# A graph-attention layer and a masked attention layer on one core: where the first layer's result is turned, which sums the q, k, v products share, and when the adjacency is copied and loaded

## The chip, the cores and the metric

The kernel runs on one core of a Trainium2 chip. The metric is the device time of one execution in microseconds; lower is better. The core has a matrix engine (TensorE, PE in the profile, with its weight loads shown as PEld), a vector engine (VectorE, DVE), a scalar engine (ScalarE, ACT), GpSimd (POOL) and SyncE (SP), which here only issues transfers. Each engine takes its own instructions in order. Transfers are done by 16 shared DMA engines.

## The reference

There are N = 4096 nodes with D = 512 features, and a 0/1 adjacency matrix of 4096 x 4096, about 0.8% of it ones. Two layers are applied, each with a residual and a layer norm:

```python
# layer 0: 4 heads of width 128
support = (x @ weight) by heads
w    = leaky_relu(f1 + f2, 0.2)          # f1, f2: dot products of support with weight_u, weight_v
attn = softmax over j of w where adjacency is set
x    = layernorm(x + attn @ support + bias + x @ proj_w + proj_b)

# layer 1: 8 heads of width 64
q, k, v = x @ Wqs, x @ Wks, x @ Wvs
scores  = q k^T / 8, masked by adjacency with the diagonal set
x       = layernorm(x + softmax(scores) v Wo)
```

Everything is float32.

## The kernel before, in words

The program has four stages one after the other. TensorE is in use through all of them.

**First products (0 to about 210 us of the span).** x is loaded in groups of 512 rows, turned by VectorE in blocks of 32 x 32 (line 741: `nc.vector.transpose`), and multiplied by the two weight matrices. Since a turn in blocks of 32 leaves the features in another order over the partitions, the weights are loaded in the same order (`load_w0`).

**Layer 0 (about 210 to 1136 us).** The 4096 result rows are taken in four windows w of 1024; for each window there is a pass for each head h, and each pass has 32 units j of 128 source rows. A unit is one trip of the loop at line 1065. In it VectorE makes a tile p of 128 x 1024 weights (`front`, line 641, and, for every second unit, a bitwise AND of mask and signs at line 636, whose signs z come from ScalarE, line 625), and TensorE multiplies the eight 128-column parts of p by the head's support rows (line 1076, 16 records in a unit). `front` runs LA = 3 units ahead of the products, and p has LA + 1 = 4 buffers. z has two buffers of two units each.

Beside that runs the preparation of the next window's adjacency (`beside_unit`; u = 32 h + j counts the units of a window):
- `narrow(w + 1, c)`, a copy in DRAM of one eighth of the window from float32 to bfloat16, issued from GpSimd (line 589) after a small token that VectorE writes, which ties it to the unit;
- `turn_in0(w + 1, c)`, a transposing load of that eighth from SyncE (line 595) into `stage`, which has two buffers;
- `shrink`, four ScalarE copies to 8-bit (line 601), which free `stage`;
- `keep`, a store of the mask to DRAM for layer 1 (line 606).

In the first window `narrow` comes at u = 22 + 7c and the loads at 52 + 8c; in the later ones at 16 + 8c and 44 + 9c. `shrink` follows its load by 14 to 18 units. SyncE's queue also holds, at j = 6 of each pass, the next pass's `fr_t` and eight `sup_t` loads (lines 616 and 987, 1 MB and 2 MB).

When a window's last pass ends, its rows are closed while the next window is already running: `divide`, `add_base`, then `close` (line 1043) for the eight row tiles, at steps 12 + 3t/2 after the end (12 + 2t for the last window). A close is `bn_stats` and `bn_aggr` on VectorE (lines 511 and 513), four small GpSimd operations, and six steps later a ScalarE `normalise` and a store to `x1_d`. Eight steps after `close` (eleven in the last window) comes `turn` (line 1054): four TensorE transposes of 128 x 128 against an identity (line 1057), a ScalarE copy out of PSUM (line 1062) and a store to `x1T_d`. In the last window's passes, groups 0 and 1 of that turned result are loaded (`load_xT`), and the k weights (`load_w`).

**q, k, v (1136 to about 1434 us).** For each pair of 512-row groups (four pairs) and each of k, q, v, `gemm` multiplies a 2 x 2 block matrix of weights by a 2 x 2 block matrix of features with seven products instead of eight. Operands are sums of blocks (`of_weights`, `of_features`), and the four results are sums of the products. A product takes 3.44 us of TensorE. The products accumulate in `s_ps`, which has three buffers. Before, three of the products are copied out by ScalarE (`sb`), GpSimd makes four sums of them in each gemm (line 1214), VectorE does one copy and two final sums (lines 1238, 1245, 1253), and GpSimd makes the features' five sums for the next pair (line 1160). The scale 1/8 of the scores is put on the q weights by one ScalarE operation (line 1273).

**Layer 1 (1434 to 3348 us).** For each group of 512 query rows and each pair of heads: scores (line 1127), exp on ScalarE (line 1341), mask on VectorE (line 1344), products with v (line 1389), sums on GpSimd and by accumulating transfers (lines 1364, 1374). In the last v gemm three scores are made ahead of time (line 1227), ahead of the last product.

The schedule is written out by hand: nothing reorders instructions. `later.at(n, fn)` emits fn n steps on.

Of the kernel before, what the change touches and what calls it, by code (L numbers as in the profile page):

```python
# [18 lines left out]
P = 128  # L19
# [410 lines left out]
def tile_gat_then_masked_attention(  # L430
# [59 lines left out]
    x1_d = [dram.tile([P, D], F32, name=f"x1_d{i}") for i in range(NT)]  # L490
# [6 lines left out]
    x1T_d = [dram.tile([P, KC, G], F32, name=f"x1T_d{g}") for g in range(NG)]  # L497
# [43 lines left out]
    def wait_by_tile(name, bufs, **kw):  # L541
# [16 lines left out]
    order = (2, 3, 4, 5, 1, 6, 7)  # L558
    of_weights = {1: ((0, 0), (1, 1), ALU.add), 2: ((1, 0), (1, 1), ALU.add),
                  5: ((0, 0), (0, 1), ALU.add), 6: ((1, 0), (0, 0), ALU.subtract),  # L560
                  7: ((0, 1), (1, 1), ALU.subtract)}
    of_features = {1: ((0, 0), (1, 1), ALU.add), 3: ((0, 1), (1, 1), ALU.subtract),
                   4: ((1, 0), (0, 0), ALU.subtract), 6: ((0, 0), (0, 1), ALU.add),
                   7: ((1, 0), (1, 1), ALU.add)}
    plain_weights = {3: (0, 0), 4: (1, 1)}
    plain_features = {2: (0, 0), 5: (1, 1)}
# [3 lines left out]
    with tc.tile_pool(name="l0", bufs=NG) as l0, \  # L570
# [21 lines left out]
        def turn_in0(w, c):  # L592

            stage[w, c] = adjT_p.tile([P, CJ, W], BF16, name="stage", bufs=2)
            nc.sync.dma_start_transpose(stage[w, c], adj_d[w][c])
# [359 lines left out]
        xTs = {}  # L955

        def load_w(dst, src, c):
            nc.sync.dma_start(dst[:, c], src[:, c * P:(c + 1) * P, :].rearrange("h p k -> p h k"))

        def load_xT(g, pool=turn_p):  # L960
            xTs[g] = pool.tile([P, KC, G], F32, name="xT1", bufs=2)
            nc.sync.dma_start(xTs[g], x1T_d[g])
# [6 lines left out]
        with wait_by_tile("l0v", 2) as vp:  # L969
            pools[1] = vp, vp  # L970

            def beside_unit(w, h, j):
# [16 lines left out]
                if w + 1 < NW:  # L989
                    for c in range(NCJ):  # L990
                        first, step = (44, 9) if w else (52, 8)
                        if u == (16 + 8 * c if w else 22 + 7 * c):
                            narrow(w + 1, c)
                        if u == first + step * c:
                            turn_in0(w + 1, c)
                        if u == min(first + 20 + step * c, H0 * NT - 1):
                            keep(w + 1, c)
                        if w == 0 and u == 98 + 3 * c:
                            keep(0, c)
                        for k in range(CJ):  # L1000
                            if u == first + 14 + step * c + 4 * k // 3:
                                shrink(w + 1, c, k)
                elif u % 4 == 0 and NT <= u < NT + 4 * KC:
                    load_w(wk, wks, (u - NT) // 4)
                elif u == NT + 4 * KC + 16:
# [576 lines left out]
```

## Time and profile before

The medians and lines are from three timed runs and one profiled execution.

| what | value |
|---|---|
| median of 3 runs (lowest to highest) | 3350.9 us (3349.1 to 3351.21) |
| profiled execution, its own time | 3350.18 us |
| its span, first to last instruction | 3348.4 us |
| mean granted TensorE clock | 0.998 |
| TensorE busy | 3325.1 us, 99% of the span |
| VectorE, ScalarE, GpSimd busy | 70%, 59%, 66% |
| chain that ended last, layer 0's products (L1076) | 27.1% |
| the same, layer 1's products (L1389) and scores (L1127) | 25.9% and 25.8% |
| the same, q, k, v (L1192 and L1185) | 5.5% and 2.7% |
| the same, TensorE's turn of the first layer's result (L1057) | 0.4% |

A busy share is an average over the stages. What an edit is worth is read from the stage that it is in: which engine has no gap there, and what is ready how long before it is needed. Times of matmuls in the profile overlap, since they are pipelined; what one of them adds to the sequence is read from the chain, where each piece starts where the one before it ends.

### The profile page before, as it was taken

What the parts mean: (1) busy time and instruction counts of PE and PEld (TensorE: products, weight loads), DVE (VectorE), ACT (ScalarE), POOL (GpSimd) and SP (SyncE); (2) the same over time, 40 slices, a digit from 0 to 9 for tenths busy, and PEclk for the clock granted to TensorE, in tenths of its full rate; (3) what the DMA queues carried; (4) which work ended last, traced back from release to release, by engine and by line L of the source; (5) the groups of instructions that cost most, each with busy time, mean ns of one, the idle gap of its engine ahead of it and who ended that gap; (6) DMA issues with size and microseconds to landing.
All of it is one profiled execution on the core that took longest, in us unless ns stands there. A gap on an engine that the chain in (4) does not pass through costs nothing.

```text
span 3348.4 us, 66683 instructions
## 1 busy us (share of the span) xinstructions
PE 3325.1 (99%) x27096; PEld 1953.1 (58%) x27096; DVE 2359.6 (70%) x2894; ACT 1986.6 (59%) x2463; POOL 2218.8 (66%) x1588
## 2 busy tenths in 40 slices
PE   9999999999999999999999999999999999999998
PEld 8899999999999755643333333333333333333332
DVE  6689899898999611167776667676666666667676
ACT  1366977878776421256666656566565656656564
POOL 5631040040020365589999999999999999999996
PEclk9999999999999999999999999999999999999999
DMA  8988869589531443379899998889988889887984
GB/s 181 229 191 163 241 152 200 145 197 186 149 105 64 117 160 114 135 204 211 199 209 220 223 208 187 212 195 245 212 191 211 192 204 255 189 211 187 212 195 112
DMA packets 399054, 620.41 MB, mean 185 GB/s; under 512 B 166672, under 2 KB 247568, under 8 KB 397712
## 3 DMA queue, kind: packets, MB, share of 16 engines
q0 software_dynamic: 97520, 258.77, 42.5%
q1 hardware_dynamic: 299344, 354.26, 34.8%
q8 instruction: 215, 3.52, 0.4%
q10 hardware_dynamic: 1872, 3.02, 0.3%
q14 instruction: 103, 0.84, 0.1%
HBM read 315.87 MB, written 117.64 MB: 129 GB/s over the span
## 4 chain that ended last, share of the span: by engine, by line
PE 96%; POOL 1%; DVE 1%; issue 1%; DMA 1%; ACT 0%; SPq 0%; POOLq 0%; ACTq 0%; DVEq 0%
PE o_ps L1076 27%; PE o_ps L1389 26%; PE s_ps L1127 26%; PE s_ps L1192 5%; PE o_ps L847 4%; PE s_ps L1453 3%; PE s_ps L1185 3%; PE s_ps L1408 1%; PE x_ps L1057 0%; DMA p<-p 0%; DVE p L1521 0%; POOL q_sum L1364 0%; POOL s L700 0%; PE x_ps L1185 0%; DVE prod L818 0%
## 5 line engine op out<-in xcount | busy, mean ns | idle before, releaser
L1364 POOL TENSOR_TENSOR q_sum<-q_sum,p 128x1024 f32<-128x1024 f32 x538 | 1374.9, 2556 | 63.0 <-DMA p<-p 39.2
L1344 DVE TENSOR_TENSOR p<-s_ps,adjT 128x1024 f32<-128x1024 f32 x896 | 1043.8, 1216 | 465.3 <-ACT s_ps L1341 436.5
L1341 ACT ACTIVATE s_ps<-s_ps 128x1024 f32<-128x1024 f32 x1021 | 967.1, 1006 | 594.5 <-PE s_ps L1127 594.3
L1389 PE MATMUL o_ps<-p,v_sb 64*64 64x512 f32 x8192 | 943.6, 590 | 0.0
L1127 PE MATMUL s_ps<-q_sb,k_sb 64*64 64x512 f32 x8192 | 942.8, 589 | 0.2 <-DVE p L1344 0.2
L1076 PE MATMUL o_ps<-sup_t,p 128*128 128x129 f32 x8192 | 919.4, 275 | 1.2 <-DVE p L641 1.2
L1076 PEld LDWEIGHTS o_ps<-sup_t,p 128*128 128x128 f32 x8192 | 917.0, 192 | 1.6 <-DVE p L641 1.4
L641 DVE SCALAR_TENSOR_TENSOR p<-fr_t,dj,az 128x1024 f32<-128x1024 f32 x512 | 652.8, 1284 | 80.4 <-PE o_ps L1076 53.1
L1389 PEld LDWEIGHTS o_ps<-p,v_sb 64*64 64x64 f32 x8192 | 310.3, 133 | 570.6 <-issue 560.3
L1127 PEld LDWEIGHTS s_ps<-q_sb,k_sb 64*64 64x64 f32 x8192 | 312.8, 133 | 566.1 <-issue 456.1
L625 ACT ACTIVATE z<-fr_t,f 128x1024 fp8e4<-128x1024 f32 x512 | 558.0, 1144 | 119.4 <-DVE az L636 119.0
L1374 POOL DMA_DIRECT2D p<-p x412 | 437.2, 1297 | 10.2 <-PE o_ps L1389 8.5
L1040 POOL DMA_DIRECT2D agg<-base_d x32 | 28.7, 1206 | 516.0 <-ACT agg L1026 515.8
L1344 DVE TENSOR_TENSOR p<-s_ps,md 128x1024 f32<-128x1024 f32 x128 | 150.7, 1217 | 68.3 <-ACT s_ps L1341 63.6
L588 POOL COPY seen<-token 128x1 f32<-128x1 f32 x24 | 13.6, 565 | 252.9 <-DVE token L586 252.9
L636 DVE TENSOR_TENSOR az<-adjT,z 128x512 int32<-128x512 int32 x256 | 175.5, 686 | 2.1 <-ACT z L625 1.4
L1199 ACT ACTIVATE sb<-s_ps 128x1024 f32<-128x1024 f32 x35 | 35.8, 1024 | 192.6 <-PE s_ps L1192 129.8
L601 ACT ACTIVATE adjT<-stage 128x1024 fp8e4<-128x1024 bf16 x128 | 130.6, 1051 | 9.5 <-DMA stage<-adj_d 9.5
L1214 POOL TENSOR_TENSOR sb<-sb,sb 128x1024 f32<-128x1024 f32 x36 | 84.9, 2373 | 72.2 <-ACT sb L1199 72.2
L1238 DVE COPY k_sb<-s_ps 128x1024 f32<-128x1024 f32 x12 | 14.7, 1225 | 141.0 <-PE s_ps L1192 91.3
L1453 PE MATMUL s_ps<-wo_sb,on 128*128 128x512 f32 x240 | 110.8, 604 | 0.0
L1423 ACT ACTIVATE r<-r_h 32x256 f32<-32x256 f32 x248 | 102.3, 412 | 2.9
(179 smaller groups left out, 2139.4 us busy)
## 6 DMA issues: line engine op xcount, KB each, us to landing
p<-p POOLq DMA_DIRECT2D x412, 512.0 KB, 9.0
k_sb<-k_d SPq DMA_DIRECT2D x128, 512.0 KB
v_sb<-v_d SPq DMA_DIRECT2D x128, 512.0 KB
adj_d<-in_adj_dram POOLq DMA_DIRECT2D x32, 1024.0 KB, 10.9
sup_t<-sup_d SPq DMA_DIRECT2D x120, 258.0 KB
fr_t<-fr_d SPq DMA_DIRECT2D x16, 1024.0 KB
adjT_d<-adjT SPq DMA_DIRECT2D x32, 512.0 KB
adjT<-adjT_d SPq DMA_DIRECT2D x32, 512.0 KB
```

Source lines behind the costliest of these rows:

```text
L625: nc.scalar.activation(z[:, k, :], fr_t[w, h][:, 0, :], AF.Sign, bias=fs[j // GT][:, 0, (j + k) % GT, h:h + 1], saturate=False)
L636: nc.vector.tensor_tensor(az.bitcast(I32), adjT[w, j // CJ][:, j % CJ:j % CJ + 2, :].bitcast(I32), z.bitcast(I32), op=ALU.bitwise_and)
L641: nc.vector.scalar_tensor_tensor(p, fr[:, 1, :], dj[j // GT][:, j % GT, h:h + 1], az_t[w, h, j // 2][:, j % 2, :], op0=ALU.max, op1=ALU.mult)
L1076: nc.tensor.matmul(o[t // BK][:, t % BK, :], p[:, t * P:(t + 1) * P], s, start=(j == 0 and t % BK == 0), stop=(j == NT - 1), skip_group_ch ...
L1127: nc.tensor.matmul(s[c:c + MS, e, :], k[r, a + c:a + c + MS], qt[g, m][r, :], start=True, stop=True)
L1192: nc.tensor.matmul(half, a[:, c, n * P:(n + 1) * P], x[:, c, :], start=not more and c == 0, stop=c == 1, skip_group_check=True)
L1341: nc.scalar.activation(s, s, AF.Exp)
L1344: nc.vector.tensor_tensor(p, s, keep[:, None, :].to_broadcast([P, HP, G]), op=ALU.mult)
L1364: nc.gpsimd.tensor_tensor(q, q, p, op=ALU.add)
L1374: later.at(2, lambda: nc.gpsimd.dma_start(a, b, accum_op=ALU.add))
L1389: nc.tensor.matmul(o[c, n, :], v[r, j % CH, c], p[r, e, :], start=(j == 0), stop=(j == NT - 1))
L1453: nc.tensor.matmul(s, on_t[g][:, m, t * P:(t + 1) * P], wo_sb[:, m, :], start=(m == 0), stop=(m == NP1 - 1))
```

## The change

**The turn.** TensorE's transposes, their copies out of PSUM and `x1T_d` are gone. The normalised rows are stored to `x1_d`, one DRAM tile for a group. `load_x1` reads a half group (256 rows) back with four transfers of 32 partitions, and `turn_x1` turns it on VectorE with four operations of 128 x 256 in blocks of 32. For groups 0 and 1 this happens in the last window's passes (loads at u = 64, 76, 88, 100; sixteen turns from u = 72, one in three units); for the others in the k, q and v gemms of the pair ahead. The k, q and v weights are loaded in the matching order: sixteen transfers in place of four for each, for k one in each unit from u = 32.

**The sums.** The seven products are those of the form with shared sums: each later operand sum is built on an earlier one, and the results share the running sum `u2`. There are four weight sums (before five) and four feature sums (five). For each gemm ScalarE copies three tiles out, VectorE makes four sums, GpSimd one (before four). The next pair's feature sums move from GpSimd to VectorE. The first product of all, and product 7 of the last gemm, use the two `x_ps` tiles. The scale 1/8 moves into the exp. The v weights are loaded after the first k gemm.

**The adjacency.** `narrow` comes at u = 16 + 5c (first window) or 13 + 5c, and the transposing loads at 50 + 8c or 48 + 8c, so that the last narrow is issued before, or one unit after, the first load. Each load of a later window waits for a two-element VectorE memset in its tile. `shrink` follows its load by 8 to 12 units, `keep` by 15.

```diff
-    order = (2, 3, 4, 5, 1, 6, 7)
...
+    order = (1, 5, 2, 6, 7, 3, 4)
+    of_weights = {5: ((1, 0), (1, 1), ALU.add), 6: (5, (0, 0), ALU.subtract),
+                  7: ((0, 0), (1, 0), ALU.subtract), 3: ((0, 1), 6, ALU.subtract)}
+    of_features = {5: ((0, 1), (0, 0), ALU.subtract), 6: ((1, 1), 5, ALU.subtract),
+                   7: ((1, 1), (0, 1), ALU.subtract), 4: ((1, 0), 6, ALU.subtract)}
+    plain_weights = {1: (0, 0), 2: (0, 1), 4: (1, 1), 7: (1, 0)}
+    plain_features = {1: (0, 0), 2: (1, 0), 3: (1, 1)}
...
             stage[w, c] = adjT_p.tile([P, CJ, W], BF16, name="stage", bufs=2)
+            if w:
+                nc.vector.memset(stage[w, c][:, 0, 0:2], 0.0)
             nc.sync.dma_start_transpose(stage[w, c], adj_d[w][c])
...
+        def load_w(dst, src, c, a):
+            f = a * P + c * SQ
+            nc.sync.dma_start(dst[a * SQ:(a + 1) * SQ, c],
+                              src[:, f:f + SQ, :].rearrange("h p k -> p h k"))
+
+        def load_x1(g, n, pool=turn_p):
...
+            if n == 0:
+                xTs[g] = pool.tile([P, KC, G], F32, name="xT1", bufs=2)
+            ys[g, n] = turn_p.tile([P, HG // SQ, P], F32, name="y1_sb", bufs=2)
+            for a in range(NQ):
+                nc.sync.dma_start(
+                    ys[g, n][a * SQ:(a + 1) * SQ],
+                    x1_d[g][n * HG:(n + 1) * HG, a * P:(a + 1) * P].rearrange(
+                        "(b r) f -> r b f", r=SQ))
+
+        def turn_x1(g, n, c):
+            nc.vector.transpose(
+                xTs[g][:, c, n * HG:(n + 1) * HG].rearrange("p (b r) -> p b r", r=SQ),
+                ys[g, n][:, :, c * SQ:(c + 1) * SQ])
...
-                        first, step = (44, 9) if w else (52, 8)
-                        if u == (16 + 8 * c if w else 22 + 7 * c):
+                        first, step = (48, 8) if w else (50, 8)
+                        if u == (13 + 5 * c if w else 16 + 5 * c):
                             narrow(w + 1, c)
                         if u == first + step * c:
                             turn_in0(w + 1, c)
-                        if u == min(first + 20 + step * c, H0 * NT - 1):
+                        if u == first + 15 + step * c:
                             keep(w + 1, c)
...
-                            if u == first + 14 + step * c + 4 * k // 3:
+                            if u == first + 8 + step * c + 4 * k // 3:
                                 shrink(w + 1, c, k)
-                elif u % 4 == 0 and NT <= u < NT + 4 * KC:
-                    load_w(wk, wks, (u - NT) // 4)
-                elif u == NT + 4 * KC + 16:
+                elif NT <= u < NT + KC * NQ:
+                    load_w(wk, wks, (u - NT) // NQ, (u - NT) % NQ)
+                elif u == NT + KC * NQ + CJ:
                     nc.vector.tensor_tensor(wk_low, block(wk, 1, 0), block(wk, 1, 1), op=ALU.add)
-                elif h == H0 - 1 and j in (NT // 2, NT // 2 + CJ):
-                    load_xT((j - NT // 2) // CJ)
+                elif u >= 2 * NT and u % CJ == 0:
+                    k = (u - 2 * NT) // CJ
+                    if k % 3 == 0 and k < 12:
+                        load_x1(k // 6, k // 3 % 2)
+                if w + 1 == NW and u >= 2 * NT + 8 and (u - 2 * NT - 8) % 3 == 0:
+                    k = (u - 2 * NT - 8) // 3
+                    if k < 16:
+                        turn_x1(k // 8, k // 4 % 2, k % 4)
...
-                    nc.sync.dma_start(x1_d[i], y)
+                    nc.sync.dma_start(x1_d[i // GT][i % GT * P:(i % GT + 1) * P, :], y)
                 later.at(6, normalise)
-                later.at(8 if w + 1 < NW else 11, lambda: turn(y, i))
-
-            def turn(y, i):
-                p = xp.tile([P, KC, P], F32, name="x_ps")
-                for c in range(KC):
-                    nc.tensor.transpose(p[:, c, :], y[:, c * P:(c + 1) * P], ident)
-                later.at(2, lambda: turned(p, i))
...
+                def add(dst, t):
+                    n = 2 * G // len(t)
+                    for k, src in enumerate(t):
+                        part = slice(k * n, (k + 1) * n)
+                        nc.vector.tensor_tensor(dst[:, part], src, u2[:, part], op=ALU.add)
...
+                    if i == (7 if last else 1 if kind == "k" and pair == 0 else 0):
+                        t[i] = [xp.tile([P, GT, P], F32, name="x_ps").rearrange(
+                            "p t r -> p (t r)") for _ in range(2)]
+                    elif i in (1, 5, 6, 7):
                         t[i] = new()
                     else:
-                        t[i] = t[{4: 2, 5: 3, 7: 1}[i]]
-                    if i == 7 and last:
+                        t[i] = t[{2: 1, 3: 5, 4: 7}[i]]
+                    if i == 4 and last:
                         for n in range(3):
                             first[n] = score(0, 0, n)
-                            nc.scalar.activation(first[n], first[n], AF.Exp)
-                    product(i, t[i], more=i in (4, 5, 7))
...
+                            nc.scalar.activation(first[n], first[n], AF.Exp, scale=float(KD) ** -0.5)
+                    product(i, t[i], more=i in (2, 3, 4))
+                    if i == 1:
+                        copy(u2, t[i])
+                    elif i == 5:
+                        copy(p5, t[i])
+                    elif i == 2:
+                        copy(out["11"], t[i])
+                        store("11")
+                    elif i == 6:
+                        add(u2, t[i])
+                    elif i == 7:
+                        add(out["22"], t[i])
+                        pool(out["22"], out["22"], p5, ALU.add)
+                        later.at(1, lambda: store("22"))
+                    elif i == 3:
+                        add(out["12"], t[i])
+                        store("12")
...
+                if more:
+                    for k, n in ((5, 0), (7, 1)):
+                        beside.setdefault(k, []).append(lambda n=n: bring(n))
+                if pair == 0:
+                    beside.setdefault(4, []).append(lambda: load_all(wv, wvs))
                 gemm(wk, wk_s, "k", pair, beside)
...
+                if more:
+                    for k, fn, n in ((1, turn, 0), (5, turn, 1), (5, bring, 2), (6, bring, 3),
+                                     (4, turn, 2)):
+                        beside.setdefault(k, []).append(lambda fn=fn, n=n: fn(n))
...
-                    nc.scalar.activation(s, s, AF.Exp)
+                    nc.scalar.activation(s, s, AF.Exp, scale=float(KD) ** -0.5)
```

In `gemm`'s callers `bring(n)` is `load_x1` and `turn(n)` the four `turn_x1` of half n of the next pair. In the v gemm, `turn(3)` follows product 1 and the next pair's four feature sums follow products 5, 6, 7 and 4.

## The prediction

> **What bounds the kernel now.** I read the page's busy times, then the stages in windows, since the changed parts lie in three of them (columns: length, then busy us of PE, PEld, DVE, ACT, POOL, and clock, DMA share, GB/s):
>
> ```profile
> PE 3325.1 (99%) x27096; PEld 1953.1 (58%) x27096; DVE 2359.6 (70%) x2894; ACT 1986.6 (59%) x2463; POOL 2218.8 (66%) x1588
> 671.00:903.00 232.00, 232.00 (x2080) 232.00 (x2080) 210.41 (x241) 184.77 (x208) 40.05 (x56) 1.00 0.81 173
> 903.00:1137.00 234.00, 233.40 (x2091) 233.21 (x2089) 207.82 (x236) 151.18 (x175) 31.02 (x41) 1.00 0.32 87
> 1137.00:1210.00 73.00, 71.77 (x230) 41.88 (x231) 25.52 (x33) 22.61 (x29) 62.77 (x64) 1.00 0.60 182
> 1284.00:1356.00 72.00, 72.00 (x224) 42.37 (x223) 10.79 (x10) 12.29 (x12) 39.34 (x18) 1.00 0.33 117
> ```
>
> TensorE has no gap in layer 0's windows or in most of q, k, v. So only fewer TensorE instructions, or gaps closed or opened, move the end. VectorE is at 210 of 232 us in layer 0, the nearest rival; in q, k, v it is nearly idle, and GpSimd is the busy helper there. Next, what the removed transposes weigh, from the chain in order of time (start, length, what), and TensorE's waits in q, k, v (total us, times, longest).
>
> ```profile
> 495.10 210.84 PE o_ps L1076 x1888
> ...
> 705.94 0.44 PE x_ps L1057 x4
> 706.37 1.79 PE o_ps L1076 x16
> 708.16 0.44 PE x_ps L1057 x4
> 708.60 3.58 PE o_ps L1076 x32
> ```
>
> ```profile
> PE s_ps L1192 <- ACT agg L1026: 1.1, 1, 1.1
> PE s_ps L1192 <- POOL adjT L1156: 0.7, 1, 0.7
> ```
>
> Four transposes take 0.44 us of the sequence, and a unit of layer 0 (16 records) 1.787 us: 118 of them, 1888 records, take 210.84. The group's row mean of 273 ns for one transpose is its pipelined duration, not its cost. Just before and beside them VectorE does the window's closes. I followed its timeline from the last p that waits for TensorE, through the closes, to the next that does:
>
> ```profile
> 677.98 2.48 DVE L641 SCALAR_TENSOR_TENSOR p<-fr_t,dj,az 128x1024 f32<-128x1024 f32 x2
> 681.16 1.28 DVE L641 SCALAR_TENSOR_TENSOR p<-fr_t,dj,az 128x1024 f32<-128x1024 f32 x1
> ...
> 689.89 1.29 DVE L641 SCALAR_TENSOR_TENSOR p<-fr_t,dj,az 128x1024 f32<-128x1024 f32 x1 [0.30 <-PE o_ps L1076]
> 691.10 0.69 DVE L511 BATCH_NORM_STATS2 bn_st<-agg 128x6 f32<-128x512 f32 x1
> 691.82 0.18 DVE L513 BATCH_NORM_AGGREGATE bn_mv<-bn_st 128x2 f32<-128x6 f32 x1
> ...
> 714.39 2.49 DVE L641 SCALAR_TENSOR_TENSOR p<-fr_t,dj,az 128x1024 f32<-128x1024 f32 x2
> ...
> 729.13 1.28 DVE L641 SCALAR_TENSOR_TENSOR p<-fr_t,dj,az 128x1024 f32<-128x1024 f32 x1 [0.70 <-PE o_ps L1076]
> ```
>
> Two units of VectorE's own work take 3.18 us (677.98 to 681.16) against TensorE's 3.57: a slack of 0.19 us a unit. Eight closes at about 0.8 us bring 6.4 us into eleven units, so from 691 to 729 VectorE never waits: its lead is being eaten.
>
> **What the Trainium skill says.** "TensorE: Matmul & The Clock Gate", Part 4, gives about 275 ns for a transpose in a kernel's context, with a copy out of PSUM after it: the rows here have 273 ns and 587 ns for that copy, though back to back a transpose costs 109. "VectorE: DVE Perf Modes", The three transpose paths, says VectorE turns only 32 x 32 blocks and stays in SBUF: hence the weights' new order. "GPSIMD Engine Reference", 4.1, puts two-input elementwise work at about twice VectorE's time: 2373 ns (L1214) against 1225 (L1245) agrees. "DMA: Bandwidth & Descriptors", Rules for kernel authors, says that all queues share and interleave on 16 engines: the transposing loads hold SyncE's queue 12 to 16 us beside narrowing copies and about 4 without, which agrees.
>
> **The turn.** Removed: 32 tiles of 4 transposes, 32 x 0.4375 = 14.0 us, 10.5 in layer 0 (three windows of 8) and 3.5 in q, k, v. The 32 ScalarE copies of 587 ns and 32 stores lay beside TensorE; they give nothing.
>
> But in layer 0 the transposes also gave VectorE time. At 689.86 TensorE ends a unit and frees the p buffer; fourteen more units, 25.02 us, and it wants the p begun at 714.39, ready about 1.25 later at 715.64. Without transposes it wants it at 714.88: 0.76 late. With the four transposes before it (1.75) there was 0.99 to spare. The same sum gives 0.75 (482.18 against a wait at 457.66) and 0.70 (946.54, 922.07) for the other windows. So 2.2 us come back: three waits on p. If ScalarE, freed of its copies, or a shifted order saves them, nothing comes back; if the extra narrow that now falls among the closes delays GpSimd's factors and with them ScalarE's signs, all of 10.5 may. I take 2.2.
>
> Added on VectorE in the last window: sixteen turns of 128 x 256. First-stage rows of that shape have 413 ns: 6.6 us in 46 units with 8.7 us of slack, one in three units, far from the closes: nothing. Uncovered they'd cost 6.6. Behind a turn in VectorE's queue is the next p, so a late load would count; each is issued eight units (14 us) ahead, where the DMA share is 0.03 to 0.25. The sixteen k loads (256 KB in 64 KB pieces, one a unit) end five units, 9 us, before `wk_low` needs them; a stall there would be at most a few us past the lead of about 4.
>
> For the other groups, 3 x 4 halves: a load comes six products (20 us) or five (17) before its turn, against 1 MB loads before; about 0.45 us of SyncE for each of four transfers. SyncE can stand behind a store of block 22 for VectorE's and GpSimd's sums, 1.2 + 2.4 us; covered.
>
> **The sums.** TensorE still has seven products of 3.44 us. In each gemm GpSimd goes from four sums of 2.37 to one, VectorE to four of 1.225 us: 4.9, plus turns 16 x 0.41 = 6.6 and feature sums 4 x 1.2 to 1.9 for a pair, some 28 us of 72. A tile in `s_ps` or under an accumulation is needed one product (3.44) after its reader starts; the worst queue, a feature sum at up to 3.4 us beside GpSimd and then a 1.2 us sum, has two products. So nothing, down to the single waits:
> - the start: product 1 needs only plain blocks and the free x_ps tiles, so the 1.1 us wait for the divides goes. Product 5, 3.44 us later, needs one VectorE sum (1.2 us after the inversions, which end 0.4 after TensorE) and all divides (about 2 us). Gain 1.1;
> - the q weights' sums come ten us ahead of use on a lighter GpSimd; the 0.7 us wait goes. The v weights, now sixteen loads of about 0.5 us at the end of the first k gemm, have a gemm (24 us). Gain 0.7;
> - the end: the second early score takes the tile of products 5 and 3, whose 1.3 us VectorE sum starts only when product 3 ends; one score takes 0.92. Loss 0.45.
>
> The exp's scale and the dropped q scaling (1.9 us of ScalarE, off the path) give nothing.
>
> **The adjacency.** No TensorE gap comes from it before, so it can't gain. A narrowing alone uses some 7 us of all engines; at a piece per five units (8.9 us) with two 3 MB batches they finish about ten units late, into the first two transposing loads. After that a load takes 4 us:
>
> ```profile
> L595 SPq DMA_TRANSPOSE stage<-adj_d x32: 3934/6508/15887, 78.3 to 860.4; - x32
> ```
>
> (minimum, median, maximum ns.) `shrink` comes 8 units, 14.3 us, after it. The memset is 0.06 us; the `shrink` it follows precedes signs that VectorE has already used, so it holds nothing. Cost nothing, given that cover.
>
> **Sum.** 3350.2 - 14.0 + 2.2 - 1.1 - 0.7 + 0.45 = 3337.1 for the profiled execution; the median of the runs lies 0.7 above it: **3337.8 us**, 0.4% faster.
>
> **Rivals.**
> - *The closes swallow layer 0's gain* (0.08): VectorE, not TensorE, paces each window's start. All 10.5 us come back in place of 2.2: 3346. For it: 9.7 of 10 us busy there; against: the sum above closes at 0.8.
> - *No wait on p at all* (0.09): ScalarE and GpSimd ease VectorE by 0.8 us a window: 3335.6.
> - *Late masks, slower* (0.08). `shrink` stands in ScalarE's queue ahead of the signs, the signs ahead of p. If each load took the longest 15.9 us, eight of them and two 7 us batches on SyncE need 141 us where eight spacings give 114; 27 late, less a lead of about 11 (z's four units and VectorE's 4 us), is 16 in each of three windows: 3386. The gain is used up from 4.4 us a window, loads of 14.5 us on average. For it: `shrink` had 14 units, now 8; against: loads without narrows take 4.
> - *Late halves of x1* (0.05): each of twelve stalling VectorE by 1 us past cover: 3350.
>
> **How the numbers follow.** 0.70 is for the forecast, within 3334 to 3342. A difference of 0.2% (6.7 us) is about what a measurement tells from none. Faster takes the forecast, the 0.09 and half of the first rival: 0.83; same, the rest of that and the x1 rival: 0.09; slower 0.08. The range, 3332 to 3346, leaves out the last two.
>
> **What would show it.** No x_ps transposes on TensorE; waits of p of some 0.8 us at 482, 714 and 945 less the shift; no wait at the start of the gemms, one of about 0.4 before the early scores; SPq's transposing loads mostly near 4 us. A ScalarE wait on `stage` followed by VectorE waits on z would make it wrong, and so would TensorE gaps on feature sums.

## The result and the profile after

The changed kernel takes 3369.67 us (median of four executions, 3364.66 to 3371.13) against 3351.06 us for the kernel before on the same chip. The ratio is 1.0053, with a 95% interval of 1.0036 to 1.007: **0.5% slower**, where 0.4% faster was forecast and 3332 to 3346 us was the range. The profiled execution is the one of 3364.66 us, 14.5 us above the profiled one of before. It is the fastest of the four; what the other three lost beyond it, 3.6 to 6.5 us, no profile shows.

The page's head, and the same stages in windows (length, then busy us of PE, PEld, DVE, ACT, POOL, and clock, DMA share, GB/s), after the change:

```profile
span 3362.9 us, 66520 instructions
PE 3315.7 (99%) x26968; PEld 1941.8 (58%) x26968; DVE 2403.6 (71%) x3005; ACT 1955.5 (58%) x2419; POOL 2105.1 (63%) x1535
```

```profile
438.00:671.00 233.00, 219.62 (x1947) 219.05 (x1947) 199.26 (x239) 174.33 (x195) 42.87 (x56) 0.98 0.76 158
671.00:903.00 232.00, 221.67 (x1962) 221.09 (x1961) 201.12 (x240) 174.64 (x196) 42.85 (x56) 0.98 0.78 164
903.00:1137.00 234.00, 233.18 (x2086) 232.80 (x2085) 218.27 (x253) 155.12 (x171) 30.70 (x40) 1.00 0.27 73
1284.00:1356.00 72.00, 72.00 (x225) 42.34 (x224) 24.59 (x32) 9.21 (x9) 7.90 (x3) 1.00 0.40 117
```

TensorE is less busy in total than before (3315.7 against 3325.1 us), as the removed transposes demand. The last row is as planned too: in q, k, v TensorE has no gap, VectorE went from 10.8 to 24.6 busy us, GpSimd from 39.3 to 7.9. But windows 1 and 2 of layer 0 now have gaps of 13.4 and 10.3 us on TensorE, and a clock of 0.98; before they had none (the prediction shows window 2, and this is window 1). Window 3 has 0.8.

```profile
438.00:671.00 233.00, 233.00 (x2089) 233.00 (x2089) 211.31 (x242) 184.77 (x208) 40.06 (x56) 1.00 0.81 173
```

The chain in order of time (start, length, what) shows what those gaps are made of. This is window 1:

```profile
493.47 27.47 PE o_ps L1085 x244
520.94 25.98 DMA stage<-adj_d
546.93 1.06 ACT adjT L600
547.99 2.09 ACT z L624 x2
550.10 0.70 DVE az L635
550.90 1.29 DVE p L640
552.24 47.78 PE o_ps L1085 x411
```

The chain leaves TensorE for the transposing load that SyncE issued at 520.94. It landed at 546.91. `shrink` (L600) waited for it, the signs z stood behind `shrink` in ScalarE's queue, `az` and p followed on VectorE, and TensorE could go on only then. In window 2 the same chain begins with a load at 765.52 that takes 22.92 us.

TensorE's timeline gives the waits (the bracket is the idle time before, and what ended it):

```profile
481.96 10.99 PE L1085 MATMUL o_ps<-sup_t,p 128*128 128x129 f32 x96 [0.81 <-DVE p L640]
493.47 46.72 PE L1085 MATMUL o_ps<-sup_t,p 128*128 128x129 f32 x416 [0.52 <-DVE p L640]
552.24 8.03 PE L1085 MATMUL o_ps<-sup_t,p 128*128 128x129 f32 x55 [12.04 <-DVE p L640]
...
793.76 6.41 PE L1085 MATMUL o_ps<-sup_t,p 128*128 128x129 f32 x37 [9.00 <-DVE p L640]
...
968.66 11.54 PE L1085 MATMUL o_ps<-sup_t,p 128*128 128x129 f32 x101 [0.81 <-DVE p L640]
```

The waits of 0.81 us are the forecast's waits on p. Those of 12.04 and 9.00 us are the late loads. And ScalarE's wait, with SyncE's own record of all loads (minimum, median and maximum ns for which one holds the queue):

```profile
PE o_ps L1085 <- DVE p L640: 25.7, 8, 12.0
ACT adjT L600 <- DMA stage<-adj_d: 49.5, 11, 20.0
```

```profile
L594 SPq DMA_TRANSPOSE stage<-adj_d x32: 3832/4947/14819, 76.9 to 876.0; - x32
```

The median of the loads, 4.9 us, is even shorter than before (6.5), and the longest no longer (14.8 against 15.9). The mean of the loads has fallen too, from 7.65 to 6.28 us, and does not show the fault: only the first two of window 1 (13.95 and 14.82 us), the first two of window 2 (12.81 and 10.95) and one ahead of layer 0's windows (10.99 at 214.69; the kernel before has 11.86 there) are over 10 us. And SyncE's record understates them: SyncE was done with the first at 534.9, but its data were there only at 546.9.

**Where the 14.5 us come from**, stage by stage, each from the start of one piece of TensorE's sequence to the start of another:

| stage | before | after | difference |
|---|---|---|---|
| to the end of layer 0's products | 1136.4 | 1154.59 | +18.2 |
| from there to the second early score | 297.8 | 292.05 | -5.7 |
| the rest, layer 1 | 1914.2 | 1916.3 | +2.0 |

Of the 2.0 us in layer 1, 0.9 are waits on p there (1.4 in place of 0.5 us); the rest was not traced.

### The profile page after: what moved, and what is told of

It is laid out like the page before. It is cut to its first block, busy times and chain, and to the rows that moved or that the text cites. A ratio compares the mean times of both kernels' runs of the same rounds, so it can differ in the third digit from the quotient of the medians.

```text
span 3362.9 us, 66520 instructions
## 1 busy us (share of the span) xinstructions
PE 3315.7 (99%) x26968; PEld 1941.8 (58%) x26968; DVE 2403.6 (71%) x3005; ACT 1955.5 (58%) x2419; POOL 2105.1 (63%) x1535
## 4 chain that ended last, share of the span: by engine, by line
PE 88%; POOL 5%; DMA 4%; DVE 2%; issue 1%; ACT 0%; POOLq 0%; SPq 0%; DVEq 0%
PE o_ps L1422 24%; PE s_ps L1136 24%; PE o_ps L1085 23%; PE s_ps L1206 6%; PE o_ps L846 4%; PE s_ps L1486 3%; PE s_ps L1199 3%; DMA p<-p 1%; DMA stage<-adj_d 1%; POOL q_sum L1397 1%; POOL bn_rs L516 1%; PE s_ps L1441 1%; DVE p L640 0%; DMA y_sb<-in_x_dram 0%; POOL bn_ve L514 0%
## 5 line engine op out<-in xcount | busy, mean ns | idle before, releaser
L600 ACT ACTIVATE adjT<-stage 128x1024 fp8e4<-128x1024 bf16 x128 | 130.9, 1051 | 49.5 <-DMA stage<-adj_d 49.5
L1228 POOL TENSOR_TENSOR k_sb<-k_sb,p 128x1024 f32<-128x1024 f32 x12 | 30.7, 2559 | 193.7 <-DVE k_sb L1234 187.9
L1213 ACT ACTIVATE u<-s_ps 128x1024 f32<-128x1024 f32 x11 | 11.3, 1023 | 174.2 <-PE s_ps L1206 110.9
L1234 DVE TENSOR_TENSOR u<-s_ps,u 128x1024 f32<-128x1024 f32 x12 | 14.7, 1225 | 107.7 <-PE s_ps L1206 77.8
```

## The experiments

The theory after the first reading: the adjacency's new schedule makes the first transposing loads of windows 1 and 2 land late, and ScalarE, VectorE and TensorE wait behind them in turn. The rival: the loads are late because of what the rest of the change does around them (no TensorE transposes, no stores of the turned result in SyncE's queue), and the schedule is not at fault. Within the theory there are three suspects: the bunched narrows beside a load, the memset that holds the load, and `shrink`'s shorter margin. Below, u counts the units of a window as in the diff, a narrow is the copy in DRAM issued by GpSimd, and a load is the transposing one from SyncE.

**1. Which part of the change makes it slower?** In the first run the changed kernel has the adjacency's whole old schedule (narrows at 16 + 8c, loads at 44 + 9c, shrink 14 units later, no memset). In the second the kernel before has the new schedule and nothing else of the change.

```diff
 after -> e1_old_adjacency
-            if w:
-                nc.vector.memset(stage[w, c][:, 0, 0:2], 0.0)
...
-                        first, step = (48, 8) if w else (50, 8)
-                        if u == (13 + 5 * c if w else 16 + 5 * c):
+                        first, step = (44, 9) if w else (52, 8)
+                        if u == (16 + 8 * c if w else 22 + 7 * c):
...
-                        if u == first + 15 + step * c:
+                        if u == min(first + 20 + step * c, H0 * NT - 1):
...
-                            if u == first + 8 + step * c + 4 * k // 3:
+                            if u == first + 14 + step * c + 4 * k // 3:
...
 before -> e2_adjacency_alone: the same lines the other way round
```

> The changed kernel with the adjacency's whole schedule of before (narrow, transposing loads, shrink, keep at their old units, no memset). Theory A (the narrowing copies, issued in a bunch, are still being worked off when the first transposing load of a window starts; that load takes 23 to 26 us, shrink is due after 14.3, and TensorE stands 12.0 and 9.0 us): all of it goes, 3337 to 3340 us, with only the three waits on p of 0.8 us in layer 0. Rival B (the turn on VectorE or the shared sums cost the time): 3365 to 3370, as the changed kernel.

> The kernel before with the adjacency's new schedule and the memset alone. Theory A: the same two waits of some 9 to 12 us and the lowered clock after them, 21 + 3 us and up to 6 more in other executions: 3373 to 3383 us. Rival B: 3351 us, no wait.

Measured: the new schedule alone costs the kernel before 19.7 us: 3370.62 us, ratio 1.0059 [1.0042, 1.0076], a little under its forecast of 3373 to 3383, with TensorE waits of 7.4 us in window 1 and 4.8 in window 2 and a first load that holds SyncE for 18.6 us. So the adjacency edit by itself makes the kernel slower by as much as the whole change does. But the first run missed its forecast: with the old schedule the changed kernel takes 3376.24 us, 1.0066 [1.0046, 1.0087]. Its loads:

```profile
L592 SPq DMA_TRANSPOSE stage<-adj_d x32: 3911/6508/25541, 80.1 to 895.2; - x32
```

In window 1 the first three hold SyncE for 25.5, 25.5 and 21.5 us, where in the kernel before the first three took 12.7, 4.05 and 6.6 with the same code. So the old schedule was not safe either, and a wider spacing of the narrows does not by itself keep the loads short: in the changed kernel this schedule has loads longer than any that the kernel before has with it. Undoing the edit is no cure, and it took other runs to find what is common to both.

**2. The wait that the memset adds, and the margin of `shrink`.** The memset holds each load until VectorE comes to it. One run takes it away, another leaves it and gives `shrink` four units more (7.1 us).

```diff
 after -> e3_no_memset
-            if w:
-                nc.vector.memset(stage[w, c][:, 0, 0:2], 0.0)
 after -> e4_later_shrink
-                        if u == first + 15 + step * c:
+                        if u == first + 17 + step * c:
...
-                            if u == first + 8 + step * c + 4 * k // 3:
+                            if u == first + 12 + step * c + 4 * k // 3:
```

> The changed kernel without the memset before the transposing loads. SyncE may then issue a window's first load as soon as its queue reaches it, at about 504 us in place of 521. If what counts is when the load is let go (A1): it lands by about 530, shrink waits 0 to 3 us on ScalarE, no TensorE wait over 1 us, 3338 to 3342 us. If the narrowing copies hold it whatever its start (A2), it takes 35 us or more and lands when it did, near 545: 3362 to 3370 us. Rival B: as A2 in time, but with no wait on stage.

> The changed kernel with shrink 12 units after its load in place of 8 (keep at 17): 7.1 us more for each load. Theory A: the two waits of 12.0 and 9.0 us fall by 7.1 each, to about 4.9 and 1.9, and the clock is not lowered: 3350 to 3356 us. Rival B: no change, 3365 to 3370.

Without the memset: 3358.42 us, 1.0019 [1.0012, 1.0026], between the two theories. The first load of window 1 goes out at 508.96 instead of 520.94 and holds SyncE for 26.7 us: longer, but begun so much earlier that it lands at 541.8. With `shrink` later: 3354.12 us, 1.0011 [1.0004, 1.0018], as forecast. But the waits of 4.9 and 1.9 us on which that forecast rested did not come: in its profile TensorE's waits in window 1 are down to 1.3 us, none of them for a load, and window 2 still has 10.0. Its first loads landed 18.8 and 29.9 us after their issue, where those of the changed kernel took 26.0 and 22.9. So the time came out partly by luck.

The two runs show how much of a late load reaches TensorE. Here are ScalarE's first `shrink` of window 1 and of window 2 without the memset (the bracket is ScalarE's wait for the load):

```profile
541.77 1.06 ACT L598 ACTIVATE adjT<-stage 128x1024 fp8e4<-128x1024 bf16 x1 [11.12 <-DMA stage<-adj_d]
779.80 1.06 ACT L598 ACTIVATE adjT<-stage 128x1024 fp8e4<-128x1024 bf16 x1 [13.52 <-DMA stage<-adj_d]
```

TensorE's longest waits in those windows are 3.2 and 5.5 us: 7.9 and 8.0 less. In the changed kernel ScalarE waits 20.02 and 16.96, TensorE 12.04 and 9.00, again 8.0 less; with the new schedule alone 15.81 and 13.18 against 7.4 and 4.8, 8.4 less. With the later `shrink` ScalarE waits 6.11 in window 1, and TensorE has no wait from it; in window 2 ScalarE waits 17.20 and TensorE 5.74, and 2.88 a little earlier, for which the profile names no cause. So for the first late load of a window z's and p's buffers cover some 8 us of ScalarE's wait, and every us beyond it is TensorE's. When the next load is late too, less is covered: in window 1 of the changed kernel with the old schedule ScalarE waits 12.73, 7.98 and 11.57 us for three loads in a row, and TensorE 4.30, 2.34 and 10.06. The kernel before has such waits too, of 4.07 in window 1 and 3.20 in window 2:

```profile
563.00 11.92 SPq L595 DMA_TRANSPOSE stage<-adj_d  x1
587.29 2.00 ACT L601 ACTIVATE adjT<-stage 128x1024 fp8e4<-128x1024 bf16 x2 [4.07 <-DMA stage<-adj_d]
```

They lie inside the 8 us, which is why its TensorE shows nothing. The first line is the load that this wait is for: it landed 24.3 us after its issue, nearly as late as the one of 26.0 in the changed kernel, and twice its hold of SyncE's queue.

**3. The cause: narrows and a transposing load in flight together.** Two runs take the overlap away from opposite sides. One moves the loads (and with them `shrink` and `keep`) eight units later, so that all narrows of the window have landed. The other keeps the loads where the change puts them and leaves out the narrowing copies of the later windows; its loads read the first window's narrowed copy, so the adjacency in the later windows is not theirs.

```diff
 after -> e6_apart
-                        first, step = (48, 8) if w else (50, 8)
+                        first, step = (56, 7) if w else (58, 7)
 after -> e7_no_narrow
-            nc.sync.dma_start_transpose(stage[w, c], adj_d[w][c])
+            nc.sync.dma_start_transpose(stage[w, c], adj_d[0][c])
...
-                            narrow(w + 1, c)
+                            pass
```

> The changed kernel with the transposing loads at 56 + 7c (first window 58 + 7c) in place of 48 + 8c (50 + 8c), shrink and keep following them as in the changed kernel; narrow stays. The first load starts 14 us later, when the narrowing copies (the last issued at 521 in the changed kernel, some 11 us from issue to landing) should be done. Theory A (a load and a narrowing copy in flight together slow each other to about 100 GB/s): every load 4 to 8 us, no TensorE wait over 1 us in layer 0, 3336 to 3342 us. If loads are slow by themselves: no gain, 3365 to 3370.

> The changed kernel with the narrowing copies of the three later windows left out; their loads read the first window's narrowed adjacency in place of their own, so that layer 0's later windows and the masks of layer 1 are computed from the wrong adjacency. The work of all engines but the narrowing is the same. Theory A: all loads 4 to 8 us, no wait but the 0.8 us ones on p (the 0.5 us after GpSimd's narrow goes too), 3335 to 3340 us. If the loads are slow for another reason, the waits of 9 to 12 us stay: 3360 and more.

Measured: 3340.53 us for the first, 0.9969 [0.9959, 0.998]; 3342.46 for the second, 0.9977 [0.9967, 0.9987]. Both cure it. SyncE's loads in the first and in the second:

```profile
L594 SPq DMA_TRANSPOSE stage<-adj_d x32: 3896/4388/11030, 76.8 to 853.4; - x32
```

```profile
L594 SPq DMA_TRANSPOSE stage<-adj_d x32: 3931/4214/10630, 78.1 to 850.8; - x32
```

In window 1 no load of either holds SyncE for more than 6.3 us; the load at 520.56 of the run without narrows, issued within 0.4 us of the one that took 13.95 us on SyncE and 26.0 to land in the changed kernel, takes 4.13 and lands after 6.2. (The maxima of 11.03 and 10.63 us are the load at about 215 us again.) Layer 0 ends at 1129.30 and 1129.49. The second run's missing 2 us (its own forecast ended at 3340) lie after layer 0: its last matmul ends 1.0 us later than that of the run with the later loads, and its span 4.5 us later. That is not explained here.

What the overlap looks like in windows of 4 us, the changed kernel and then the one with the loads later (columns as above):

```profile
522.00:526.00 4.00, 4.00 (x38) 4.00 (x38) 3.90 (x4) 3.00 (x4) 0.24 (x1) 1.00 1.28 149
526.00:530.00 4.00, 4.00 (x39) 4.00 (x38) 3.65 (x5) 0.92 (x1) 0.00 (x0) 1.00 1.31 59
...
534.00:538.00 4.00, 4.00 (x38) 4.00 (x37) 0.38 (x2) 0.00 (x0) 0.00 (x0) 1.00 1.31 110
...
542.00:546.00 4.00, 0.00 (x0) 0.00 (x0) 0.00 (x0) 0.00 (x0) 0.00 (x0) 0.92 1.38 103
```

```profile
522.00:526.00 4.00, 4.00 (x38) 4.00 (x37) 3.90 (x5) 3.00 (x4) 0.18 (x1) 1.00 0.97 145
526.00:530.00 4.00, 4.00 (x38) 4.00 (x37) 3.66 (x5) 3.00 (x3) 0.00 (x0) 1.00 0.96 156
530.00:534.00 4.00, 4.00 (x38) 4.00 (x37) 3.60 (x4) 2.23 (x3) 0.00 (x0) 1.00 0.04 6
534.00:538.00 4.00, 4.00 (x38) 4.00 (x38) 3.61 (x6) 2.19 (x2) 0.00 (x0) 1.00 0.64 137
```

Up to 522 us the two kernels have issued the same narrows at the same times (the last at 521.49 and 521.43). Alone, what is left of them is over by about 530, and a load issued then, at 534.36, takes 4.03 us. With the load among them from 520.94 on, the DMA engines show a share of 1.3 for over 20 us while only 59 to 149 GB/s are moved. Both are slow: the load lands after 26.0 us, and the narrow issued at 521.49 after 27.1. Following one another in the run with the later loads, the last narrow lands 10.4 us after its issue and a load alone 6 to 9 us after its own, so that the two would have been done some 17 to 20 us after 521, by an estimate from these figures.

The DMA queues tell which of the two holds the engines (packets, MB, share of the 16 engines; q1 is SyncE's queue, with packets of the load alone, q0 GpSimd's with the narrows). First 526 to 534 us in the changed kernel, then 536 to 538 in the kernel with the later loads, where the load is alone:

```profile
q1 hardware_dynamic: 1365, 0.35, 109.0%
q0 software_dynamic: 225, 0.23, 23.2%
```

```profile
q1 hardware_dynamic: 1923, 0.49, 116.3%
```

Over 8 us on 16 engines the 1365 packets took 102 ns each; over 2 us the 1923 took 19. So a packet of the load takes five times as long beside the narrows, and it is the load's packets that fill the engines while little is moved. The overlap is the cause of the long loads in the changed kernel; why a packet then takes so long is not seen in these traces. Nor is a narrow issued near a load enough: the first window has the new schedule too, and its first load, issued at 293.05 between narrows at 286.45 and 295.65, holds SyncE for 4.00 us.

**4. The waits on p.** The prediction said that without the transposes three waits on p come back, because the closes eat VectorE's lead. If so, closes further apart (12 + 2t steps in all windows, as the last window has them) take the waits away.

```diff
 e6_apart -> e8_apart_spread
-                        later.at(12 + (3 * t // 2 if w + 1 < NW else 2 * t),
+                        later.at(12 + 2 * t,
```

> As e6_apart, and with the closes of a window every second unit (12 + 2t) in all windows. VectorE's lead over TensorE then lasts: eight closes of 0.8 us in 14 units with 0.19 us of slack each need 6.4 - 2.7 = 3.7 us of a lead of about 4. The three waits on p of 0.8 us and the 0.5 us ones go: 2 to 3.5 us less than e6_apart. If the waits don't come from the closes: no difference.

TensorE's waits on p in layer 0, first in the kernel with the later loads, then with the closes spread too:

```profile
PE o_ps L1085 <- DVE p L640: 3.5, 5, 0.8
```

```profile
PE o_ps L1085 <- DVE p L640: 1.4, 2, 1.2
```

The first row leaves out the wait of 1.2 us at the start of layer 0, which all these kernels have (there it ends at 214.3, and the rows count from 215). The second row is this wait and one of 0.2: the five others are gone. In the profiled runs layer 0 ends 2.3 us earlier, at 1127.04. The median is 3336.07 us, 4.5 less than with the later loads alone, where 2 to 3.5 were forecast; all four executions lie below all nine of that kernel. The profiles (3336.1 and 3334.0 us of span) show 2.1 of it, and the rest is not explained. At 0.9957 [0.994, 0.9973] of the kernel before this is the fastest version found: the change as made, with the loads eight units later and the closes two steps apart.

**5. What kept the kernel before out of it?** This was tried three times and not settled. First TensorE's transposes were put back beside the first three windows' closes, into the changed kernel with the old schedule; then the whole old turn, with ScalarE's copy and SyncE's store (in both the turned result isn't used). Last, the kernel before got the memset alone, which moves its loads by some us.

```diff
 e1_old_adjacency -> e5_stand_in
+                if w + 1 < NW:
+                    later.at(8, lambda: stand_in(y))
+
+            def stand_in(y):
+                p = xp.tile([P, KC, P], F32, name="x_ps")
+                for c in range(KC):
+                    nc.tensor.transpose(p[:, c, :], y[:, c * P:(c + 1) * P], ident)
 e5_stand_in -> e9_full_stand_in
+    x1T_d = [dram.tile([P, KC, G], F32, name=f"x1T_d{g}") for g in range(NG)]
...
-                    later.at(8, lambda: stand_in(y))
+                    later.at(8, lambda: stand_in(y, i))
...
-            def stand_in(y):
+            def stand_in(y, i):
...
+                later.at(2, lambda: stood_in(y, p, i))
+            def stood_in(y, p, i):
+                x1T = y.rearrange("p (c r) -> p c r", c=KC)
+                nc.scalar.activation(x1T, p, AF.Copy)
+                nc.sync.dma_start(x1T_d[i // GT][:, :, i % GT * P:(i % GT + 1) * P], x1T)
 before -> e10_before_held
+            if w:
+                nc.vector.memset(stage[w, c][:, 0, 0:2], 0.0)
```

> The changed kernel with the adjacency's old schedule, and with TensorE's transposes put back at their old places in the three first windows, their results unused (24 of the 32 tiles, 10.5 us of TensorE). It tells why the old schedule, free of collisions in the kernel before, collides in the changed one. Theory T (only the moment counts: the transposes spread the units by 3.5 us a window, and without them the loads fall onto the narrowing copies): the loads are short again, 3350 to 3356 us although TensorE has more to do. Theory U (something else that the turn's change took away or moved in memory): the loads stay at 20 us and more, 3370 to 3390.

> The changed kernel with the adjacency's old schedule and the whole old turn (TensorE's transposes, ScalarE's copy, SyncE's store) put back beside the first three windows' closes; the turned result isn't used. Theory M (what kept the old schedule's loads short was the stores in SyncE's queue, which let the first transposing load of a window out only at about 510 us instead of 503 to 507): the load goes out at 509 or later and none of windows 1 and 2 stands over 18 us in SyncE's queue; 3345 to 3356 us. Theory N (something else, VectorE's or GpSimd's moments, decides): loads of 20 us and more as in the run with the transposes alone, 3360 to 3380.

> The kernel before, whose transposing loads of the later windows each wait for a two-element VectorE memset in their tile, as the changed kernel's do; nothing else is changed. If the kernel before stands at the edge of the same collision, moving its loads by some us makes first loads of 18 us and more and gaps on TensorE: 3356 to 3372 us. If it is robust to the moment of the loads: 3348 to 3354.

Transposes alone: 3362.11 us, 1.0042 [1.0024, 1.0059], with executions at 3360 to 3362 and two near 3376, the profiled one among these; the first load at 503.0, and the first three at 17.8, 26.7 and 23.3 us. The time falls between the two theories; the loads of its profile stay at 20 us and more, as the theory says by which the transposes are not what mattered. The whole turn: 3355.64 us, 1.001 [1.0002, 1.0018], inside what the theory of the stores expects, but the profiled execution (3365.77 us) contradicts its mechanism: the first load goes out at 511.09, later than in the kernel before, and takes 13.66 us (12.66 there); but the second, at 524.8, takes 26.5 us, where the one of before took 4.05 at 522.8. In it window 2 has no gap at all. The kernel before with held loads: 3352.97 us, 1.0009 [1.0001, 1.0018]; in its profile the first load goes out at 514.63, the longest holds SyncE for 18.8 us, and TensorE has no gap in windows 1 and 2. But that profile is of its fastest execution (3348.61 us). Four of the fourteen took 3357 to 3360 us, where the kernel before beside them stayed within 3348.84 to 3355.05, and one took 13323.82. So the kernel before bears a shift of its loads by 4.6 us in most executions (for the four slower ones it is not shown), and the moment of the first load does not decide by itself.

Nor does the overlap as such: in the kernel before, the first load's packets beside a narrow (516 to 520 us) take 34 ns each, by this line over 4 us, against 102 in the changed kernel.

```profile
q1 hardware_dynamic: 764, 0.20, 40.8%
```

The kernel before meets the costly form as well, but later in the window and inside its cover: its fourth and fifth loads, at 563.00 and 577.65, hold SyncE for 11.92 and 15.37 us. Why its first three escape it, and those of the changed kernel with the same schedule do not, stays open.

## Why the prediction was wrong

**The step that failed is "The adjacency": "Cost nothing, given that cover".** The working there was right in its first half: the narrows do run late, into the first two loads of windows 1 and 2, and the later loads do hold SyncE for about 4 us. Wrong was what an overlapped load costs. The 12 to 16 us of the kernel before are what it holds SyncE's queue, and they were taken for its time to landing. In the changed kernel the first load landed after 26.0 us, 12 us after SyncE was free of it; and in the kernel before one had landed after 24.3 us with a hold of 11.9.

Two more terms were off. `shrink` was taken to come 14.3 us, eight units, after its load. But the memset ties the load to VectorE (it runs at 520.84, the load goes out at 520.94), and ScalarE runs ahead of VectorE: it had reached its `shrink` at 526.9, 6.0 us after the load. So "it holds nothing" failed as well: without the memset the same load went out 12.0 us earlier. And the lead behind ScalarE is 8 us, not about 11. With these the loss comes out: 26.0 - 6.0 - 8.0 = 12.0, which is the wait that the profile shows. (The 8.0 is read from this wait and found again in the run without the memset.)

In the kernel before, the lateness lay inside the lead: there, too, a stretch of 10 us at a DMA share of 1.33 moves only 91 GB/s, and loads hold SyncE for 15 us and land after 24, but `shrink` came fourteen units after a load that nothing tied to VectorE. The row of loads was read as a duration and not as a warning.

The rival *late masks, slower* (0.08) had the mechanism and the place. Its price had the wrong form: a mean over eight loads, with a threshold of 14.5 us. Here the mean of the loads is well under that, and one late load is enough, since nothing behind it can be earlier than its landing; nor does the loss add up over the eight loads, so the 3386 us were too many.

**What the gaps cost beyond themselves.** Against the version with the later loads, layer 0 ends 25.3 us later (1154.59 - 1129.30). TensorE's waits account for 13.4 - 1.3 and 10.3 - 1.3, 21.1 us. Most of the other 4.2 is the granted clock, in the changed kernel's windows of 2 us:

```profile
544.00:546.00 2.00, 0.00 (x0) 0.00 (x0) 0.00 (x0) 0.00 (x0) 0.00 (x0) 0.85 1.31 110
546.00:548.00 2.00, 0.00 (x0) 0.00 (x0) 0.00 (x0) 1.06 (x2) 0.00 (x0) 0.50 1.30 81
...
552.00:554.00 2.00, 1.76 (x8) 1.76 (x9) 1.38 (x2) 2.00 (x3) 0.00 (x0) 0.50 0.03 8
554.00:556.00 2.00, 2.00 (x13) 2.00 (x13) 1.82 (x2) 2.00 (x4) 0.00 (x0) 0.59 0.09 35
556.00:558.00 2.00, 2.00 (x21) 2.00 (x20) 1.95 (x3) 2.00 (x3) 0.00 (x0) 1.00 0.55 227
```

TensorE stopped at 540.2; the clock fell to 0.50 near 545.4 and came back near 555.6, 3.4 us after the products went on. Busy time at the lower clock is lost in proportion: 1.76 x 0.50 + 2.0 x 0.41 = 1.7 us, and 2.1 by the same sum in window 2. The Trainium skill, "TensorE: Matmul & The Clock Gate", HAM oscillation — how this bites in real kernels, warns of idle gaps of more than about 3.4 us; the trace agrees, since both gaps are longer, but in window 2 the clock fell already 3.0 us after the stop (5.2 in window 1).

**The turn: right.** In the version with later loads layer 0 ends 7.1 us earlier than before (1136.4 - 1129.30). The forecast has -10.5 for 24 tiles and +2.2 for waits on p. The three waits came at 0.81, 0.81 and 0.81 us (0.75, 0.76 and 0.70 forecast). Not foreseen in size were a second of 0.52 in each of windows 1 and 2: -10.5 + 2.4 + 1.0 = -7.1. These are the narrows among the closes, which the step named as a danger: GpSimd issues one at 483.02, ahead of the last close's four small operations, and the signs behind that `normalise` come late. In the run without narrows the 0.52 are gone and the 0.81 remain, and with the closes spread both are gone. VectorE's sixteen turns and the reloading of x1 cost nothing that shows.

**The sums: right, and a little better.** From the end of layer 0 to the second early score the forecast has -3.5 - 1.1 - 0.7 + 0.45 = -4.85 us; measured are -5.7. The waits for the divides and for the q weights' sum are gone. The wait of 0.45 before the second early score did not come: between the two scores lie 3.65 us of the last product, as before the change. The remaining 0.4 us were not traced.

**The sum.** Forecast for the profiled execution was 3337.1 us. With the overlap taken out, and nothing else of the change touched, 3337.97 were profiled. The other terms held to within 1.2 us each, and the close agreement is partly luck, since their errors cancel: the turn gave 7.1 us in place of 8.3, the sums 5.7 in place of 4.85, and layer 1 took 0.5 more. The median of that version, 3340.53 us, lies 2.6 above its profiled execution, where 0.7 was assumed. The term that was set to nothing was worth 27 us between the profiled executions (3364.66 - 3337.97) and 29 between the medians (3369.67 - 3340.53). Too much confidence was put on it: it was the only edit in which a margin was cut (`shrink` from 14 units to 8) while copies were bunched ahead of the transfer that it waits for, and its cost was bounded by SyncE's holds in the kernel before. Those bound it for that kernel alone: the changed kernel with the very same schedule has holds of 25.5 us.

## What to carry to other kernels

A duration taken from a transfer beside others holds for those others only, and here not even for the same schedule in the changed kernel. Price a load that runs into other copies at its landing, not at its queue's hold, and set against that the moment at which its reader's own engine gets there, which may run ahead of the engine that lets the transfer go. Look for one late transfer, not for the mean: an engine that takes its work in order passes on the latest landing, and everything behind it waits. When two streams make one another slow, moving the later one until the first has landed can be free, as the eight units here were, and the rest of an otherwise good change can then be had.

## What the runs showed of the hardware

- A transposing load from SyncE (1 MB) alone holds the queue for about 4 us and lands 6 to 9 us after its issue. Together with narrowing copies from GpSimd the slowed loads of windows 1 and 2 in the changed kernel held it for 11 to 15 us and landed after up to 26.0; in the other kernels holds reached 27 us and one landing took 39.4 (with the whole old turn put back, 524.84 to 564.23). The engines showed a share of about 1.3 while 59 to 149 GB/s were moved, and a packet of the load took 102 ns in place of 19. Alone, a load moved 260 GB/s over 522 to 526 us in the run without narrows. The Trainium skill, "DMA: Bandwidth & Descriptors", Rules for kernel authors, says that "A transpose next to ordinary DMAs needs nothing"; that sentence stands beside one on transposes that corrupt one another and gives no time, and these runs show that in time such a neighbour can cost much.
- SyncE's hold on its queue and the landing of the transfer can be far apart: 13.95 and 26.0 us for the same load, and 11.92 and 24.3 for one of the kernel before.
- TensorE's clock fell to 0.50 in gaps of 9.0 and 12.0 us, 3.0 and 5.2 us after the stop, and came back 4.2 and 3.4 us after the restart. In these runs a gap of 3.2 us (without the memset, window 1) lowered it too; one of 2.9 (later `shrink`, window 2) did not.
